# Attention and mixture-of-experts block on one core: value product in pieces of 256 queries, two query tiles less lag, last head's output kept in SBUF, more output projection inside the last head

## The chip, the cores and the metric

One NeuronCore of a Trainium2 chip runs the whole program. The metric is the device time of one execution in microseconds (us); the median of several executions counts. The engines run side by side and meet only at semaphores: TensorE (PE) multiplies matrices into PSUM, VectorE (DVE) and ScalarE (ACT) read PSUM and SBUF, GpSimd (POOL) reads and writes SBUF only, and SyncE (SP) issues DMAs. ACT and POOL issue DMAs too.

## The reference

2048 tokens of 256 features pass through an attention layer with 16 heads of 128 and through a layer of 8 experts with the best 2 chosen for each token. Cut to what matters:

```python
x = x + ln(attn(ln(x)))
x = x + ln(moe(ln(x)))

def attn(x):                       # codes * scales give the weights
    q, k, v = x @ Wq + bq, x @ Wk + bk, x @ Wv + bv       # 16 heads of 128
    p = softmax(q @ k.T / sqrt(128))                       # per head 2048 x 2048
    return concat_heads(p @ v) @ Wo + bo

def moe(x):                        # 8 experts, 176 hidden features each
    w = combine(top2(softmax(x @ Wr)))
    return sum_e w[:, e] * ((silu(x @ Wg[e]) * (x @ Wu[e])) @ Wd[e])
```

The result has to be accurate to float32, so each operand that is stored in 16 bits is stored twice, as a high part and as a low part (the rest), and a product is made of three: high by high, high by low, low by high.

## The kernel before

The order of the work on each engine is written out by hand: an instruction runs on its engine in the order in which the code emits it. SP's queue is such an order too, and a DMA that waits holds up those behind it.

**Start.** x is normalized, transposed and split; the first head's q, k and v projections begin. Projections write a PSUM bank of the tags "pj" or "pv" (`psA`, one bank each) or one of three "s" slots (`psS`). `proj_v(p, t0, n, tag, wide)` (L248 on) projects n tiles of V for head pair p. Without `wide` ACT copies the high part out of PSUM and DVE subtracts it from PSUM for the low part (L266, L267), so the bank stays taken until DVE is done. With `wide` ACT copies the bank to an SBUF tile `t32` (L274) and POOL makes both parts from that (L275, L276). `proj_qk` (L222 on; L237, L238, or L243 to L245) has the same two ways.

**Main loop.** A step g is one head h and one tile t of 128 queries: 16 x 16 = 256 steps and two more. In a step PE makes the scores of its tile in two halves (`scores_half`, L508 to L512, six matmuls of 512 columns each), DVE takes the maximum (L513, L517), ACT the exponentials p with their sums (L524). One step later DVE makes the reciprocal (L531, L534), ACT the scaled high part ph (L538), DVE the low part pl in two halves (L553). SP transposes ph and pl by DMA into `pth` and `ptl` (L541, L559), whose tiles hold four query tiles each, with two buffers of each.

**Value product.** For a head and a block b of 512 queries `pv_part` (L571 on) issues 48 matmuls of 512 columns into one PSUM bank, first the 32 that read `pth`, then the 16 that read `ptl`. They are cut into 8 units of 6, and each step runs two units (`pv_unit`). `PVLAG` (13) is the lag: unit u of the loop is unit u - PVLAG of the value product, so the first unit runs in step 6.5, and 9 units are left over when the loop ends. The finished bank goes through `t32` to POOL, which splits it into the tile `o` and writes it by DMA to `ot_d[b]` in DRAM (L594 to L599). Only the last head's last block is split by ACT and DVE.

**Fill.** At the end of a step `fill(h, t)` adds one projection for a coming head: q and k at even t, V at odd t. In the last head there is nothing left to project but three blocks of q.

**Output projection and the end.** `op_mm(b, half, js)` (L712 on) multiplies stored head outputs, read back with `load_oi` in groups of four heads (0.5 MB), by Wo: 16 matmuls of 256 columns for each group j. In the last head `early` and `late` place these loads on ACT's queue, the groups of block 0 between the steps, and the loads and splits of the gate weights. Block 0's layer norms (`ln_a`, `ln_b1`, `ln_b2`, `ln_c`, DVE and POOL) come after the loop, together with block 1's projection, block 0's router and the splits of the up and down weights. The slots for these loads, for V, K, ph, pl and the loaded weights all come from one pool of `NX` (21) slots with the tag "x".

**Feed-forward.** Four blocks of 512 tokens, each 11 chunks: gate and up products (`gate_up`, L987), then `down` (L1027). The layer norms and the router of a later block, and the projections of blocks 2 and 3, are placed between the chunks (`FIRST`, `PREP`, `PREP2`).

Of the kernel before, what the change touches and what calls it, by code (L numbers as in the profile page):

```python
# [32 lines left out]
PS = 16384.0  # L33
NX = 21


@with_exitstack
def sandwich(
# [26 lines left out]
    dram = ctx.enter_context(tc.tile_pool(name="dram", bufs=1, space=DRAM))  # L65
    ot_d = [dram.tile([128, 2, NH, 2, 256], HP, name=f"ot_d{b}") for b in range(4)]

# [427 lines left out]

    pt = pt_ctx.enter_context(tc.tile_pool(name="pt", bufs=2, reuse_waits="tile"))
    soft = soft_ctx.enter_context(tc.tile_pool(name="soft", bufs=2, reuse_waits="tile"))
# [38 lines left out]
    def high_part(h, t, m, p):  # L536
        ph = kqv.tile([128, S], HP, name="ph", tag="x", bufs=NX)
        nc.scalar.activation(ph, p, AF.Copy, scale=m[:, 6:7])  # L538
        if t % 4 == 0:
            PT[(h, t // 4)] = pt.tile([128, 4, 16, 128], HP, name="pth")  # L540
        nc.sync.dma_start_transpose(  # L541
            out=PT[(h, t // 4)][:, t % 4], in_=ph
        )
        return ph
# [3 lines left out]
    def low_half(half, h, t, m, p, ph):  # L548
        if half == 0:
            LOW[(h, t)] = kqv.tile([128, S], HP, name="pl", tag="x", bufs=NX)  # L550
        pl = LOW[(h, t)]
        cs = bass.ts(half, 1024)
        nc.vector.scalar_tensor_tensor(  # L553
            pl[:, cs], p[:, cs], m[:, 6:7], ph[:, cs], ALU.mult, ALU.subtract
        )
        if half == 1:
            if t % 4 == 0:
                PTL[(h, t // 4)] = pt.tile([128, 4, 16, 128], HP, name="ptl")
            nc.sync.dma_start_transpose(  # L559
                out=PTL[(h, t // 4)][:, t % 4], in_=LOW.pop((h, t))  # L560
            )
# [9 lines left out]
    def pv_part(h, b, e):  # L571
        if e == 0:
            pvps[(h, b)] = psA.tile([128, 512], F32, name="pv")
        ps = pvps[(h, b)]
        dc = bass.ts(h % 2, 128)
        for n in range(6 * e, 6 * e + 6):
            c, i = PV_ORDER[n]
            d = (PTL if i == 2 else PT)[(h, b)]
            nc.tensor.matmul(  # L579
                ps, V[(h // 2, c // 4)][:, i % 2, c % 4, dc], d[:, :, c, :],  # L580
                start=(n == 0), stop=(n == 47),
            )
        if e == 7:
            if (h, b) == (NH - 1, 3):
                o = kqv.tile([128, 2, 2, 256], HP, name="o_last", tag="x", bufs=NX)
                ps2 = halves(ps)
                nc.scalar.activation(o[:, :, 0, :], ps2, AF.Copy, scale=1.0 / PS)
                nc.vector.scalar_tensor_tensor(
                    o[:, :, 1, :], ps2, 1.0 / PS, o[:, :, 0, :], ALU.mult, ALU.subtract
                )  # L590
            else:
                o = soft.tile([128, 2, 2, 256], HP, name="o", bufs=1)
                t32 = soft.tile([128, 512], F32, name="t32")
                nc.scalar.activation(t32, ps, AF.Copy, scale=1.0 / PS)  # L594
                nc.gpsimd.tensor_copy(o[:, :, 0, :], halves(t32))
                nc.gpsimd.tensor_tensor(  # L596
                    o[:, :, 1, :], halves(t32), o[:, :, 0, :], ALU.subtract
                )
            nc.gpsimd.dma_start(  # L599
                out=ot_d[b][:, :, h].rearrange("p f l q -> p f (l q)"),  # L600
                in_=o.rearrange("p f l q -> p f (l q)"),
            )

    QK = {0: ("q", 0, 1), 2: ("k", 1, 0), 4: ("q", 0, 2), 6: ("k", 1, 1),
          8: ("q", 0, 3), 10: ("k", 1, 2), 12: ("q", 1, 0), 14: ("k", 1, 3)}

    LASTQ = {0: 1, 1: 2, 4: 3}

    def fill(h, t):
        p = h // 2  # L610
        if h == 0 and t < 6:
            proj_v(0, 4 + 2 * t, 2, "pv")
        if h == NH - 1:
# [72 lines left out]
    def load_oi(b, half, j, tag="x", eng=None):  # L686
        oi = kqv.tile(
            [128, 4, 2, 256], HP, name="oi", tag=tag, bufs=NX
        )
        (eng or nc.sync).dma_start(  # L690
            out=oi.rearrange("p h l q -> p (h l q)"),
            in_=ot_d[b][:, half, 4 * j : 4 * j + 4].rearrange("p h l q -> p (h l q)"),
        )
        OIN[(b, half, j)] = oi


    PVLAG = 13
    NS = NH * NT
# [13 lines left out]
    def op_mm(b, half, js, tag="pj", part=3):  # L712
# [9 lines left out]
        for j in js:  # L722
            oi = OIN.pop((b, half, j))
            for t in range(2):
                for hh in range(4):
                    for hl in range(2):
                        nc.tensor.matmul(  # L727
                            ps[:, t], oi[:, hh, hl, bass.ts(t, 128)],
                            wo[j // 2][:, 4 * (j % 2) + hh, :],
# [47 lines left out]
    def ln_c(b):  # L777
# [3 lines left out]
    XV = x.rearrange("b (c p t) d -> p (b c) t d", p=128, t=4)  # L781
    GW_LOAD = {2: 0, 4: 1, 6: 2, 8: 3}
    GW_SPLIT = {5: 0, 7: 1, 9: 2, 11: 3}
    OI_LOAD = {
        3: (0, 1, 0), 5: (0, 1, 1), 7: (0, 1, 2), 9: (1, 0, 0), 10: (1, 0, 1),
        12: (0, 0, 3), 13: (0, 1, 3), 14: (1, 0, 2),
    }
    OI_USE = {
        5: (0, (0,)), 6: (0, (1,)), 7: (0, (2,)), 8: (1, (0,)), 9: (1, (1,)), 10: (1, (2,)),
        14: (0, (3,)), 15: (1, (3,)),  # L790
    }

    def early(t):
# [9 lines left out]
        if t == 13:  # L803
            nc.gpsimd.tensor_tensor(crow, crow, brow, ALU.add)
        if t in (8, 10, 12):
            load_oi(0, 0, t // 2 - 4, eng=nc.scalar)

    def late(t):
# [5 lines left out]
        if t in OI_USE:  # L814
            op_mm(0, *OI_USE[t], "pj", 2)
        if t in GW_SPLIT:
# [4 lines left out]
        if t in OI_LOAD:  # L821
            load_oi(*OI_LOAD[t], eng=nc.scalar)
        if t == 11:
            X1[0] = kqv.tile([128, 4, D], F32, name="x1_0", tag="x", bufs=NX)
            nc.scalar.dma_start(out=X1[0], in_=XV[:, 0])


    defer = False
    prev2 = None
    for g in range(NS + 2):  # L830
        h, t = divmod(g, NT)
        live = g < NS
# [47 lines left out]
        if g == NS:  # L880
            ln_a(0)
        if g == NS + 1:
            load_oi(1, 0, 3)
            ust = [load_gu(wu, 0, kqv, "x", NX)]
            ust += [load_gu(wu, i, kqv, "x", NX) for i in range(1, 4)]
            ln_b1(0)
    UEND = 2 * (NS + 2)


    def tr(b, kc, tag="pj"):  # L890
        xn = AT[b]
        if kc == 0 and b == 0:
            XT[b] = [
                kqv.tile([128, 2, 512], F32R, name="xT0", tag="x", bufs=NX)
                for _ in range(2)
            ]
        elif kc == 0:
# [11 lines left out]
    def router_a(b, tag="pj"):  # L909
# [9 lines left out]
        if b == 0:  # L919
            LGT[b] = kqv.tile([8, 512], F32, name="lgT0", tag="x", bufs=NX)  # L920
        else:
# [24 lines left out]
    def router_c(b):  # L946
# [174 lines left out]
    op_mm(1, 0, (3,), "s")  # L1121
    for j in range(4):
        load_oi(1, 1, j)
    router_a(0, "s")
    for e in range(5, 7):
        pv_unit(UEND + e)
    split_gu(uw, 2, ust[2], True)
    router_b(0, "s")
    split_gu(uw, 3, ust[3], False)
    for e in range(7, 9):  # L1130
        pv_unit(UEND + e)
# [3 lines left out]
    router_c(0)  # L1135
# [101 lines left out]
```

## Time and profile before

| | |
|---|---|
| runs | 1825.22, 1827.94, 1835.36 us; median 1827.94 |
| profiled execution | 1829.47 us, its span 1827.6 us |
| mean granted PE clock | 0.994 |
| score matmuls (L508, L509, L512) | 3072 of 128x512, 379 ns each |
| value matmuls (L579) | 3072 of 128x512, 379 to 381 ns each |
| output projection matmuls (L727) | 512 of 128x256, 273 ns each |
| weight loads of the value product | 3072, 98 ns each |
| transposes on SP (L541, L559) | 256 and 256, 5.1 and 5.3 us from issue to landing (median) |
| reads of stored head outputs | 32 of 512 KB |

The profile of one execution gives for each engine its busy time, in groups of instructions by line, and in order of time. A matmul's duration there (379 ns) is longer than its share of the engine, since matmuls overlap; how fast PE works is read from the distance between starts. The page's second part cuts the span into 40 slices of some 46 us, one digit each for the busy share. A wait is told as the instruction that stood still, and the one that released it. The main loop runs from about 30 to 1560 us, the feed-forward from about 1590 to the end.

### The profile page before, as it was taken

The numbers are of one execution on the slowest core, as the hardware profiler recorded it, in microseconds if no ns is written. First come the engines' busy times: TensorE is split into PE (matmuls) and PEld (weight loads), VectorE is DVE, ScalarE is ACT, GpSimd is POOL, SyncE is SP. The second block draws the span as 40 slices with busy tenths as digits, with TensorE's granted clock in tenths as the row PEclk, the third lists the DMA queues.
The fourth block names the chain that finished last, engine by engine and source line by source line (L and its number), as shares of the span: only waits on it lengthen the run. The fifth ranks groups of instructions, "written<-read, shape, count | busy, mean of one in ns | idle before, by whom it ended". The sixth has DMA issues, their size and how long they took to land. (4 is left out here: it accounts for less than half of the span.)

```text
span 1827.6 us, 25508 instructions
## 1 busy us (share of the span) xinstructions
PE 1775.5 (97%) x8890; PEld 934.1 (51%) x8890; DVE 1631.0 (89%) x2269; ACT 1371.5 (75%) x1732; POOL 946.9 (52%) x915
## 2 busy tenths in 40 slices
PE   6899999999999999999999999999999998999997
PEld 4344444444444444444444444444444454688886
DVE  7999999999999999999999999999999987558666
ACT  5788888888888888888888888888888886322232
POOL 3396556555656565656565656566444332323232
PEclk9999999999999999999999999999999999999999
DMA  7999999999999999999999999999999999921000
GB/s 174 174 191 201 197 201 203 199 201 200 199 189 207 199 199 200 198 200 202 201 192 199 205 200 197 197 200 203 191 189 194 205 240 223 321 74 36 1 13 23
DMA packets 1092337, 330.70 MB, mean 181 GB/s; under 512 B 1069729, under 2 KB 1079281, under 8 KB 1092209
## 3 DMA queue, kind: packets, MB, share of 16 engines
q1 hardware_dynamic: 1077904, 293.29, 89.0%
q0 software_dynamic: 9920, 27.82, 5.5%
q10 hardware_dynamic: 4384, 7.96, 1.5%
q8 instruction: 70, 1.15, 0.2%
q14 instruction: 59, 0.48, 0.1%
HBM read 41.68 MB, written 18.87 MB: 33 GB/s over the span
## 5 line engine op out<-in xcount | busy, mean ns | idle before, releaser
L524 ACT ACTIVATE p<-s,m,ssc 128x1024 f32<-128x1024 f32 x512 | 612.2, 1200 | 190.5 <-DVE m L517 179.3
L553 DVE SCALAR_TENSOR_TENSOR pl<-p,m,ph 128x1024 f16<-128x1024 f32 x512 | 725.8, 1418 | 2.5 <-ACT ph L538 2.5
L513 DVE TENSOR_REDUCE m<-s 128x1 f32<-128x1024 f32 x512 | 622.3, 1216 | 39.8 <-PE s L512 38.2
L538 ACT ACTIVATE ph<-p,m 128x2048 f16<-128x2048 f32 x256 | 512.8, 2003 | 50.5 <-ACT t L243 15.3
L579 PE MATMUL pv<-pth,v 128*128 128x512 f16 x2048 | 507.7, 381 | 15.0 <-DMA pth<-ph 6.1
L579 PEld LDWEIGHTS <-v 128*128 128x128 f16 x3072 | 300.8, 98 | 383.5 <-issue 13.9
L508 PE MATMUL s<-kT,qT 128*128 128x512 f16 x1024 | 388.5, 379 | 2.7 <-ACT p L524 2.0
L509 PE MATMUL s<-kT,qT 128*128 128x512 f16 x1024 | 388.6, 379 | 0.7 <-POOL kT L245 0.7
L512 PE MATMUL s<-kT,qT 128*128 128x512 f16 x1024 | 304.6, 379 | 0.0
L579 PE MATMUL pv<-ptl,v 128*128 128x512 f16 x1024 | 251.9, 379 | 0.0
L244 POOL CAST qT<-t 128x512 f16<-128x512 f32 x63 | 78.5, 1245 | 236.4 <-ACT t L243 236.4
L275 POOL CAST v<-t 128x256 f16<-128x256 f32 (+1 forms) x105 | 47.1, 449 | 257.2 <-ACT t L274 257.2
L276 POOL TENSOR_TENSOR v<-t,v 128x256 f16<-128x256 f32 (+1 forms) x105 | 160.6, 1530 | 8.5
L512 PEld LDWEIGHTS <-qT 128*128 128x128 f16 x1024 | 100.3, 98 | 122.0 <-issue 1.5
L509 PEld LDWEIGHTS <-qT 128*128 128x128 f16 x1024 | 100.2, 98 | 113.7 <-issue 7.5
L508 PEld LDWEIGHTS <-qT 128*128 128x128 f16 x1024 | 100.3, 98 | 109.0 <-issue 1.0
L1002 POOL TENSOR_TENSOR hh<-sg,hh 128x512 fp32r<-128x512 f32 x42 | 55.1, 1311 | 143.5 <-ACT hh L1001 108.5
L1001 ACT CAST hh<-sg 128x512 fp32r<-128x512 f32 (+1 forms) x45 | 27.5, 612 | 107.0 <-DVE sg L1013 107.0
L524 ACT ACTIVATION_READ_ACCUMULATOR p<-s,m,ssc 128x1 f32 x512 | 99.0, 193 | 0.0
L596 POOL TENSOR_TENSOR o<-t,o 128x512 f16<-128x512 f32 x63 | 94.5, 1499 | 5.2
L244 POOL CAST kT<-t 128x512 f16<-128x512 f32 x60 | 64.5, 1075 | 58.5 <-ACT t L243 53.3
L245 POOL TENSOR_TENSOR kT<-t,kT 128x512 f16<-128x512 f32 x60 | 89.8, 1496 | 5.1
(189 smaller groups left out, 1833.4 us busy)
## 6 DMA issues: line engine op xcount, KB each, us to landing
ot_d<-o POOLq DMA_DIRECT2D x63, 256.0 KB, 4.2
oi<-ot_d SPq DMA_DIRECT2D x21, 512.0 KB, 8.8
oi<-ot_d ACTq DMA_DIRECT2D x11, 512.0 KB, 4.1
pth<-ph SPq DMA_TRANSPOSE x256, 5.1
ptl<-pl SPq DMA_TRANSPOSE x256, 5.3
xt<-in_L_attn_x SPq DMA_DIRECT2D x4, 512.0 KB, 4.7
woc<-in_L_attn_wo_codes SPq DMA_DIRECT2D x4, 512.0 KB, 9.6
wos<-in_L_attn_wo_scales SPq DMA_DIRECT2D x16, 128.0 KB, 8.4
```

The lines of the kernel that those rows point to most:

```text
L244: nc.gpsimd.tensor_copy(t[:, 0, :], t32)
L245: nc.gpsimd.tensor_tensor(t[:, 1, :], t32, t[:, 0, :], ALU.subtract)
L276: nc.gpsimd.tensor_tensor(v[:, 1, sl, :], t32, v[:, 0, sl, :], ALU.subtract)
L508: nc.tensor.matmul(s[:, j, :], q[:, 0, qc], k[:, 0, :], start=True, stop=False)
L509: nc.tensor.matmul(s[:, j, :], q[:, 0, qc], k[:, 1, :], start=False, stop=False)
L512: nc.tensor.matmul(s[:, j, :], q[:, 1, qc], k[:, 0, :], start=False, stop=True)
L513: nc.vector.tensor_reduce(m[:, half : half + 1], s, AX.XY, ALU.max)
L524: nc.scalar.activation(p[:, bass.ts(i, 1024)], s, AF.Exp, bias=m[:, 2:3], scale=ssc[:, 0:1], accum_out=m[:, 3 + i : 4 + i],)
L538: nc.scalar.activation(ph, p, AF.Copy, scale=m[:, 6:7])
L553: nc.vector.scalar_tensor_tensor(pl[:, cs], p[:, cs], m[:, 6:7], ph[:, cs], ALU.mult, ALU.subtract)
L579: nc.tensor.matmul(ps, V[(h // 2, c // 4)][:, i % 2, c % 4, dc], d[:, :, c, :], start=(n == 0), stop=(n == 47),)
L596: nc.gpsimd.tensor_tensor(o[:, :, 1, :], halves(t32), o[:, :, 0, :], ALU.subtract)
```

## The change

Six things are changed together.

- The value product works on 256 queries at a time: `pth` and `ptl` tiles hold two query tiles, with three buffers of each, and the 48 matmuls of a block become twice 48 of 256 columns, into the two halves of the same PSUM bank. A unit is 12 such matmuls. `PVLAG` goes from 13 to 9 units, two query tiles.
- The last head's output is not written to DRAM. It stays in four SBUF tiles (`O15`), and the fourth read-back group holds three heads instead of four.
- In the first head six of the eight V projections use `wide`. The V projections of later pairs are placed some steps earlier.
- In the last head the projection of block 0 is done by step 11, and half of block 1's follows in steps 12 to 15, with block 0's layer norms beside it in the same steps. Loads for them are placed earlier on ACT's queue.
- The other half of block 1 runs in the two steps after the scores have ended; block 2's projection moves from the feed-forward's first block to the stretch before it. The order of the stretch between loop and feed-forward is rewritten.
- The pool "x" has 22 slots. Block 0's router and its transposed input take three of them, cleared beforehand by POOL.

```diff
-NX = 21
+NX = 22
...
-    ot_d = [dram.tile([128, 2, NH, 2, 256], HP, name=f"ot_d{b}") for b in range(4)]
+    ot_d = [dram.tile([128, 2, NH - 1, 2, 256], HP, name=f"ot_d{b}") for b in range(4)]
...
-    pt = pt_ctx.enter_context(tc.tile_pool(name="pt", bufs=2, reuse_waits="tile"))
+    pt = pt_ctx.enter_context(tc.tile_pool(name="pt", bufs=3, reuse_waits="tile"))
...
-        if t % 4 == 0:
-            PT[(h, t // 4)] = pt.tile([128, 4, 16, 128], HP, name="pth")
+        if t % 2 == 0:
+            PT[(h, t // 2)] = pt.tile([128, 2, 16, 128], HP, name="pth")
...
-        for n in range(6 * e, 6 * e + 6):
+        f = e // 4
+        for n in range(12 * (e % 4), 12 * (e % 4) + 12):
             c, i = PV_ORDER[n]
-            d = (PTL if i == 2 else PT)[(h, b)]
+            d = (PTL if i == 2 else PT)[(h, 2 * b + f)]
             nc.tensor.matmul(
-                ps, V[(h // 2, c // 4)][:, i % 2, c % 4, dc], d[:, :, c, :],
-                start=(n == 0), stop=(n == 47),
+                ps[:, bass.ts(f, 256)], V[(h // 2, c // 4)][:, i % 2, c % 4, dc],
+                d[:, :, c, :], start=(n == 0), stop=(n == 47),
             )
         if e == 7:
+            if h == NH - 1:
+                o = kqv.tile([128, 2, 2, 256], HP, name="o_last", tag="x", bufs=NX)
+                O15[b] = o
+            else:
+                o = soft.tile([128, 2, 2, 256], HP, name="o", bufs=1)
...
-            nc.gpsimd.dma_start(
-                out=ot_d[b][:, :, h].rearrange("p f l q -> p f (l q)"),
-                in_=o.rearrange("p f l q -> p f (l q)"),
-            )
+            if h < NH - 1:
+                nc.gpsimd.dma_start(
+                    out=ot_d[b][:, :, h].rearrange("p f l q -> p f (l q)"),
+                    in_=o.rearrange("p f l q -> p f (l q)"),
+                )
...
+    V0 = (6, 8, 12, 14)
...
-        if h == 0 and t < 6:
-            proj_v(0, 4 + 2 * t, 2, "pv")
+        if h == 0 and t < 4:
+            proj_v(0, V0[t], 2, "pv", wide=soft)
+            if t == 1:
+                proj_v(0, 10, 2, wide=soft)
...
-            if t in (3, 5) and h > 0:
-                proj_v(p, 12 + (t - 3) // 2, 1, wide=soft)
-            elif t == 7 and h > 0:
-                proj_v(p, 14, 2, wide=soft)
-            elif t >= 9 and p + 1 < NH // 2:
-                proj_v(p + 1, (t - 9) // 2, 1, wide=soft)
+            if t == 1 and h > 0:
+                proj_v(p, 14, 1, wide=soft)
+            elif t == 3 and h > 0:
+                proj_v(p, 15, 1, wide=soft)
+            elif t >= 5 and p + 1 < NH // 2:
+                if h > 0 or t > 7:
+                    proj_v(p + 1, (t - 5) // 2, 1, wide=soft)
+                elif t == 7:
+                    proj_v(p + 1, 0, 2, wide=soft)
         elif p + 1 < NH // 2:
-            proj_v(p + 1, 4 + t // 2, 1, wide=soft)
+            proj_v(p + 1, 6 + t // 2, 1, wide=soft)
...
-    PVLAG = 13
+    PVLAG = 9
...
     OI_LOAD = {
-        3: (0, 1, 0), 5: (0, 1, 1), 7: (0, 1, 2), 9: (1, 0, 0), 10: (1, 0, 1),
-        12: (0, 0, 3), 13: (0, 1, 3), 14: (1, 0, 2),
+        3: (0, 0, 3), 4: (0, 1, 3), 9: (1, 0, 0), 10: (1, 0, 1), 11: (1, 0, 2), 12: (1, 0, 3),
+        13: (1, 1, 0), 14: (1, 1, 1), 15: (1, 1, 2),
     }
     OI_USE = {
-        5: (0, (0,)), 6: (0, (1,)), 7: (0, (2,)), 8: (1, (0,)), 9: (1, (1,)), 10: (1, (2,)),
-        14: (0, (3,)), 15: (1, (3,)),
+        5: (0, 0, (0,)), 6: (0, 0, (1,)), 7: (0, 0, (2,)), 8: (0, 1, (0,)), 9: (0, 1, (1,)),
+        10: (0, 1, (2,)), 11: (0, 0, (3,)),
+        12: (1, 0, (0,)), 13: (1, 0, (1,)), 14: (1, 0, (2,)), 15: (1, 0, (3,)),
     }
...
+            if t == 11:
+                op_mm(0, 1, (3,), "pj", 2)
...
+        LN0 = {12: ln_a, 13: ln_b1, 14: ln_b2, 15: ln_c}
+        if t in LN0:
+            LN0[t](0)
...
                 proj_v(0, 2, 2, "pv")
+                proj_v(0, 4, 2, "s", wide=soft)
...
+        if g >= NS:
+            op_mm(1, 1, ((0, 1), (2, 3))[g - NS], "s")
...
         if g == NS:
-            ln_a(0)
+            for j in range(4):
+                load_oi(2, 0, j)
...
-    op_mm(1, 0, (0, 1, 2), "s")
-    ln_b2(0)
-    split_gu(uw, 0, ust[0], True)
-    ln_c(0)
-    for e in range(1, 5):
-        pv_unit(UEND + e)
     tr(0, 0, "s")
     tr(0, 1, "s")
+    pv_unit(UEND + 1)
+    router_a(0, "s")
+    pv_unit(UEND + 2)
+    router_b(0, "s")
+    split_gu(uw, 0, ust[0], True)
+    op_mm(2, 0, (0, 1, 2, 3), "s")
...
-    op_mm(1, 1, (0, 1), "s")
     router_d(0, "s")
     split_d(*d1)
-    op_mm(1, 1, (2, 3), "s")
+    op_mm(2, 1, (0, 1, 2, 3), "s")
...
-        3: [lambda: op_pass(2, 0, "pv")],
-        5: [lambda: tr(1, 0), lambda: op_pass(2, 1, "pv"), lambda: loads(3, 7)],
+        5: [lambda: tr(1, 0), lambda: loads(3, 7)],
```

More of the change, by code (lines that the diff above doesn't have):

```diff
@@ L538, in high_part @@
         nc.scalar.activation(ph, p, AF.Copy, scale=m[:, 6:7])
-        if t % 4 == 0:
-            PT[(h, t // 4)] = pt.tile([128, 4, 16, 128], HP, name="pth")
+        if t % 2 == 0:
+            PT[(h, t // 2)] = pt.tile([128, 2, 16, 128], HP, name="pth")
         nc.sync.dma_start_transpose(
-            out=PT[(h, t // 4)][:, t % 4], in_=ph
+            out=PT[(h, t // 2)][:, t % 2], in_=ph
         )
@@ L556, in low_half @@
         if half == 1:
-            if t % 4 == 0:
-                PTL[(h, t // 4)] = pt.tile([128, 4, 16, 128], HP, name="ptl")
+            if t % 2 == 0:
+                PTL[(h, t // 2)] = pt.tile([128, 2, 16, 128], HP, name="ptl")
             nc.sync.dma_start_transpose(
-                out=PTL[(h, t // 4)][:, t % 4], in_=LOW.pop((h, t))
+                out=PTL[(h, t // 2)][:, t % 2], in_=LOW.pop((h, t))
             )
     pvps = {}
+    O15 = {}
     def halves(t):
@@ L575, in pv_part @@
         dc = bass.ts(h % 2, 128)
-        for n in range(6 * e, 6 * e + 6):
+        f = e // 4
+        for n in range(12 * (e % 4), 12 * (e % 4) + 12):
             c, i = PV_ORDER[n]
-            d = (PTL if i == 2 else PT)[(h, b)]
+            d = (PTL if i == 2 else PT)[(h, 2 * b + f)]
             nc.tensor.matmul(
-                ps, V[(h // 2, c // 4)][:, i % 2, c % 4, dc], d[:, :, c, :],
-                start=(n == 0), stop=(n == 47),
+                ps[:, bass.ts(f, 256)], V[(h // 2, c // 4)][:, i % 2, c % 4, dc],
+                d[:, :, c, :], start=(n == 0), stop=(n == 47),
             )
         if e == 7:
+            if h == NH - 1:
[3 more added lines that the diff above has]
+                o = soft.tile([128, 2, 2, 256], HP, name="o", bufs=1)
             if (h, b) == (NH - 1, 3):
-                o = kqv.tile([128, 2, 2, 256], HP, name="o_last", tag="x", bufs=NX)
                 ps2 = halves(ps)
@@ L591, in pv_part @@
             else:
-                o = soft.tile([128, 2, 2, 256], HP, name="o", bufs=1)
                 t32 = soft.tile([128, 512], F32, name="t32")
@@ L686, in load_oi @@
     def load_oi(b, half, j, tag="x", eng=None):
-        oi = kqv.tile(
-            [128, 4, 2, 256], HP, name="oi", tag=tag, bufs=NX
-        )
+        n = 4 if j < 3 else 3
+        oi = kqv.tile([128, n, 2, 256], HP, name="oi", tag=tag, bufs=NX)
         (eng or nc.sync).dma_start(
             out=oi.rearrange("p h l q -> p (h l q)"),
-            in_=ot_d[b][:, half, 4 * j : 4 * j + 4].rearrange("p h l q -> p (h l q)"),
+            in_=ot_d[b][:, half, 4 * j : 4 * j + n].rearrange("p h l q -> p (h l q)"),
         )
-        OIN[(b, half, j)] = oi
-    PVLAG = 13
+        OIN[(b, half, j)] = [oi[:, hh] for hh in range(n)]
+    PVLAG = 9
     NS = NH * NT
@@ L723, in op_mm @@
             oi = OIN.pop((b, half, j))
+            if j == 3:
+                oi.append(O15[b][:, half])
             for t in range(2):
@@ L727, in op_mm @@
                         nc.tensor.matmul(
-                            ps[:, t], oi[:, hh, hl, bass.ts(t, 128)],
+                            ps[:, t], oi[hh][:, hl, bass.ts(t, 128)],
                             wo[j // 2][:, 4 * (j % 2) + hh, :],
@@ L781, in sandwich @@
     XV = x.rearrange("b (c p t) d -> p (b c) t d", p=128, t=4)
-    GW_LOAD = {2: 0, 4: 1, 6: 2, 8: 3}
+    EARLY = {
+        4: (0, 0, 0), 6: (0, 0, 1), 8: (0, 0, 2), 10: (0, 1, 0), 12: (0, 1, 1), 14: (0, 1, 2),
+    }
+    GW_LOAD = {0: 0, 2: 1, 6: 2, 8: 3}
     GW_SPLIT = {5: 0, 7: 1, 9: 2, 11: 3}
     OI_LOAD = {
-        3: (0, 1, 0), 5: (0, 1, 1), 7: (0, 1, 2), 9: (1, 0, 0), 10: (1, 0, 1),
-        12: (0, 0, 3), 13: (0, 1, 3), 14: (1, 0, 2),
+        3: (0, 0, 3), 4: (0, 1, 3), 9: (1, 0, 0), 10: (1, 0, 1), 11: (1, 0, 2), 12: (1, 0, 3),
+        13: (1, 1, 0), 14: (1, 1, 1), 15: (1, 1, 2),
     }
     OI_USE = {
-        5: (0, (0,)), 6: (0, (1,)), 7: (0, (2,)), 8: (1, (0,)), 9: (1, (1,)), 10: (1, (2,)),
-        14: (0, (3,)), 15: (1, (3,)),
[3 rows of a table added]
     }
@@ L804, in early @@
             nc.gpsimd.tensor_tensor(crow, crow, brow, ALU.add)
-        if t in (8, 10, 12):
-            load_oi(0, 0, t // 2 - 4, eng=nc.scalar)
+        if t in EARLY:
+            load_oi(*EARLY[t], eng=nc.scalar)
     def late(t):
@@ L814, in late @@
         if t in OI_USE:
-            op_mm(0, *OI_USE[t], "pj", 2)
+            b = OI_USE[t][0]
+            op_mm(*OI_USE[t], "pj", 2 if b == 0 else 3)
+            if t == 11:
+                op_mm(0, 1, (3,), "pj", 2)
         if t in GW_SPLIT:
@@ L822, in late @@
             load_oi(*OI_LOAD[t], eng=nc.scalar)
-        if t == 11:
+        if t == 15:
+            load_oi(1, 1, 3, eng=nc.scalar)
+        if t == 7:
             X1[0] = kqv.tile([128, 4, D], F32, name="x1_0", tag="x", bufs=NX)
             nc.scalar.dma_start(out=X1[0], in_=XV[:, 0])
+        LN0 = {12: ln_a, 13: ln_b1, 14: ln_b2, 15: ln_c}
+        if t in LN0:
+            LN0[t](0)
     defer = False
@@ L880, in sandwich @@
         if g == NS:
-            ln_a(0)
+            for j in range(4):
+                load_oi(2, 0, j)
+        if g == NS - 1:
+            rt0 = kqv.tile([128, 1024], F32, name="rt0", tag="x", bufs=NX)
+            xt0 = [
+                kqv.tile([128, 2, 512], F32R, name="xT0", tag="x", bufs=NX)
+                for _ in range(2)
+            ]
+            for z in (rt0, *xt0):
+                nc.gpsimd.memset(z.bitcast(F32), 0.0)
         if g == NS + 1:
[L883 to L886, printed above, removed]
+            ust = [load_gu(wu, i, kqv, "x", NX) for i in range(4)]
     UEND = 2 * (NS + 2)
@@ L892, in tr @@
         if kc == 0 and b == 0:
[L893 to L896, printed above, removed]
+            XT[b] = xt0
         elif kc == 0:
@@ L919, in router_a @@
         if b == 0:
-            LGT[b] = kqv.tile([8, 512], F32, name="lgT0", tag="x", bufs=NX)
+            LGT[b] = rt0[:8, :512]
         else:
@@ L957, in router_c @@
         )
-        cx = tl.tile([128, 4, 8, 16], F32, name="cx", tag="sg", bufs=3)
+        if b == 0:
+            cx = rt0[:, 512:].rearrange("p (t e r) -> p t e r", t=4, e=8)
+        else:
+            cx = tl.tile([128, 4, 8, 16], F32, name="cx", tag="sg", bufs=3)
         sx = [128, 4, 8, 16]
@@ L1111, in sandwich @@
     d1 = load_d(4)
-    op_mm(1, 0, (0, 1, 2), "s")
-    ln_b2(0)
-    split_gu(uw, 0, ust[0], True)
-    ln_c(0)
-    for e in range(1, 5):
-        pv_unit(UEND + e)
     tr(0, 0, "s")
     tr(0, 1, "s")
+    pv_unit(UEND + 1)
[4 more added lines that the diff above has]
+    op_mm(2, 0, (0, 1, 2, 3), "s")
     split_gu(uw, 1, ust[1], False)
-    op_mm(1, 0, (3,), "s")
+    split_gu(uw, 2, ust[2], True)
+    split_gu(uw, 3, ust[3], False)
     for j in range(4):
[L1123 to L1131, printed above, removed]
+        load_oi(2, 1, j)
+    pv_unit(UEND + 3)
+    router_c(0)
+    pv_unit(UEND + 4)
     pt_ctx.close()
@@ L1134, in sandwich @@
     dw = tl.tile([128, 2, NCH, D], F32R)
-    router_c(0)
     split_d(*d0)
     load_x1(1)
-    op_mm(1, 1, (0, 1), "s")
     router_d(0, "s")
     split_d(*d1)
-    op_mm(1, 1, (2, 3), "s")
+    op_mm(2, 1, (0, 1, 2, 3), "s")
     ln_a(1)
@@ L1173, in sandwich @@
     FIN = {2: fin1, 3: fin2}
-    loads(2)
     for q in range(4 * NCH + 2):
```

## The prediction

> **What bounds the kernel now.** I read busy shares first, then slices, the PE timeline at both ends, the waits, and last SP's timeline.
>
> ```profile
> PE 1775.5 (97%) x8890; PEld 934.1 (51%) x8890; DVE 1631.0 (89%) x2269; ACT 1371.5 (75%) x1732; POOL 946.9 (52%) x915
> ...
> PE   6899999999999999999999999999999998999997
> ...
> DVE  7999999999999999999999999999999987558666
> ```
>
> A busy PE need not be a full PE, so I look at spacing. In the windows view PE is busy 99.4 to 99.7 of every 100 us from 400 to 1400, and in the timeline six score and six value matmuls that start at 1520.42 give way to the next scores at 1523.01: 2.59 us for 12, so 215.8 ns each, with nothing between. In the middle every PE instruction added lengthens the kernel. DVE at 95% (190.4 of 200 us) is next. Time can be won only where PE stands still, and that is at the two ends and in one small recurring wait.
>
> At the start the PE timeline shows (start, duration, [idle before <- releaser]):
>
> ```profile
> 46.48 1.05 PE L255 MATMUL pj<-wv,xnT 128*128 128x256 bf16 x8 [1.97 <-DVE v L267]
> ...
> 53.11 1.83 PE L255 MATMUL pj<-wv,xnT 128*128 128x256 bf16 x8 [2.13 <-DVE v L267]
> ...
> 60.55 1.05 PE L255 MATMUL pj<-wv,xnT 128*128 128x256 bf16 x8 [2.13 <-DVE v L267]
> ...
> 73.42 1.47 PE L579 MATMUL pv<-pth,v 128*128 128x512 f16 x6 [1.10 <-DVE v L267]
> ```
>
> The V projection of each early tile waits until DVE has subtracted the one before out of the same PSUM bank, and no value product exists before 73.42. The eight idle stretches from 40.24 to 73.42 sum to 11.35 us. After the one at 53.11 PE runs slow for ten rows of matmuls: 1.62 us for 8 where 0.88 is usual, then 2.23 us for 6 scores where 1.29 is usual, another 1.7. Lost: **13.0 us**.
>
> At the other end:
>
> ```profile
> 1538.86 0.59 PE L512 MATMUL s<-kT,qT 128*128 128x512 f16 x2
> 1545.06 4.31 PE L579 MATMUL pv<-pth,v 128*128 128x512 f16 x12 [5.60 <-DMA pth<-ph]
> ...
> 1560.01 5.40 PE L727 MATMUL op_s<-wo,oi 128*128 128x256 bf16 x48
> 1567.83 7.03 PE L579 MATMUL pv<-pth,v 128*128 128x512 f16 x24 [2.41 <-issue]
> ```
>
> 5.60, 2.41 and three small ones (0.31, 0.85, 0.59) are 9.8 us; the 12 and the 24 matmuls behind the long gaps take 4.14 and 6.86 us to the next start where 2.59 and 5.18 are usual, 3.2 more. Lost: **13.0 us**. Why so late? SP's timeline:
>
> ```profile
> 1529.23 6.72 SPq L541 DMA_TRANSPOSE pth<-ph  x1
> 1536.05 2.72 SPq L559 DMA_TRANSPOSE ptl<-pl  x1
> 1538.87 3.30 SPq L541 DMA_TRANSPOSE pth<-ph  x1
> ```
>
> Counting back from the last one (1561.76, tile 15), the transpose at 1538.87 is tile 11's. ACT had written that ph by 1527.01, so SP is 12 us behind. From 1490 to 1538.87 SP is never free and takes 6.1 us a tile, while PE takes only 5.2 us for tiles without projection. So the transposes, beside one 0.5 MB load per tile, are what the last head runs into. "issue" at 1567.83 is, I think, the same: tile 15's transpose went out at 1561.76 and needs the usual 5 to 6 us.
>
> The recurring wait, from the waits of PE:
>
> ```profile
> PE pv L579 <- POOL v L276: 5.0, 7, 0.8
> ...
> PE pv L579 <- POOL v L275: 0.4, 1, 0.4
> ```
>
> The last V tiles of each head pair come 0.7 us too late: **5.4 us**.
>
> **The change part by part.**
>
> 1. Value product by 256. 3072 matmuls of 512 columns become 6144 of 256, each with its own weight load. Nearest row: the output projection (L727), 128x256 with a load for every matmul; 64 of them take 7.00 us in the chain of waits, 16 take 1.74 to 1.75 us in the last head. That is 109.1 ns, so a pair costs 218.2 against 215.8: 2.4 ns x 3072 = **+7.4 us**, all on PE's path. The Trainium skill speaks against this ("TensorE: Matmul & The Clock Gate", Back-to-back issue gap): in a stream of load and matmul pairs it counts about 81 ns at 128 columns where a lone matmul needs 56, because the load wants its share. That 25 ns on 256 columns would make 134 ns and +161 us (estimate from that page). The row has the same pairs at 109.1, with the load (98 ns each) hidden, and the page's 131 ns for 512 columns is not this trace's 215.8 either. I take the row. Ends: +5 (108.7 ns) to +43 us (115 ns).
>
> 2. Start. Six of the eight V projections go through ACT and POOL, so the bank is free after ACT's copy (0.58) and DVE loses 0.68 us a tile. Then the loop of exponentials 2.4, m and reciprocal 0.5, pl 1.2, reduce 1.2, maximum 0.3 gives 5.5 us a tile instead of 6.2 to 7.4 (ACT's exponentials now start at 41.71, 47.96, 54.59, 62.03). One more projection ahead of the first scores delays them 0.9. POOL gets 6 x (1.05 + 1.65) = 16.1 us, beside q and k splits of 2.6 each and weight loads; from 34 to 62 I count some 27 us, so it just keeps up. The last V tile is needed at about 66. The first value unit moves from step 6.5 to 4.5 (a step is one query tile), to about 57.5. From there PE is full: 0.86 + 5.18 + 0.86 + 4 units of 1.30 reach the old 73.42 at 69.6, so 3.8 earlier, with 4 units (5.2 us) already done. **-9.0 us**; ends -4 (POOL holds up the shared t32) and -12.
>
> 3. V of later pairs is projected so that its last tile has 1.6 steps (9 us) to its use instead of 1.0 (5.8, and 0.7 short). **-5.4 us**; ends 0 and -6. Transposes keep two steps to their first use, and those of the low part get 2.8 steps instead of 4. A third buffer frees each pair's space one step ahead. No new PE wait in the middle.
>
> 4. Last head. The projection in it grows from 8 to 12 groups of 16 matmuls (1.75 us each): PE work moved, zero by itself. But tiles 5 to 15 then last at least 6.95 us on PE, more than SP's 6.1 us, so the backlog drains rather than grows; the load at each tile from 9 on is what SP had beside it before. Head 15's write and read-back fall away; they were off the path except through DMA traffic. Two groups of 32 (3.5 us each) now stand between the last scores and tile 15's values, which PE reaches 17.6 us after the last scores (six units of 1.3, a group of 1.75, 1.1 of transposes for the router, and twice 3.5). Maximum 1.5, exponentials 2.4, reciprocal 0.4, ph 2.0 and a transpose of 5 to 9 give 11 to 15. Against it, block 0's normalization moves onto DVE: at, stats, ln_b1 3.6, ln_b2 2.2, ln_c 2.4, together 13.5 us over five tiles of 5.4 (DVE from 1518.15 to 1523.80, less 0.29 idle). DVE then needs 40.5 us where PE needs 36.5: 4 us late, and ln_c and the last statistics stand directly before tile 15's reciprocal (up to 4). On ACT's queue the last loads may also wait for a slot that a transpose must free, and ph waits behind them; four loads stand before tile 15's low transpose on SP, covered by 7 us of projection. I let 5 of the 13.0 remain: **-8.0 us**; ends -13 and +3.
>
> 5. Feed-forward. Its first block loses op_pass(2), 14 us of cover; DVE there has 2.1 us per chunk plus normalizations of 3.6, 2.2 and 2.4 in three chunks, 14.5 against PE's 12.5. **+1 us**; ends 0 and 3.
>
> Sum: 7.4 - 9.0 - 5.4 - 8.0 + 1.0 = **-14.0 us**. The profiled execution took 1829.5 (span 1827.6 and 1.9 around it), which gives 1815.5; the median of the runs is 1.5 lower, so for a median I say **1814**.
>
> **Rivals.**
> - The end does not pay: DVE or a slot takes the place of the late transpose. For it: 40.5 against 36.5 us, and the loads on ACT. Against it: the two projection groups before tile 15's values. 1814 + 8 = **1822**. Chance 0.2.
> - Start and V pay half, because ACT and DVE's loop of 5.5 us is so near PE's 5.8: 1814 + 7 = **1821**, with half of the end gone too 1825. Chance 0.09.
> - Slower: the 256-column matmuls in the main loop space wider than in L727, where the load has only 11 ns to hide in. The price is 6.1 us per ns. The other parts bring 21.4 us, so it decides from 111.4 ns; at 115 ns +43.6 - 21.4 gives **1850**. Against it: spacing in every L727 row but one. Chance 0.16, with 1835 to 1860 as its span.
>
> **How the numbers follow.** The forecast has 0.55 (1806 to 1820); less than 0.5%, 9 us, can't be told from no change. Below 1819: nearly all of the forecast and a little of the rivals, 0.56. Up to 1837: the first two rivals, 0.27. The rest, 0.17, is the slow one with an end that fails as well. Leaving out most of that rival: 1804 to 1834.
>
> **What would show it.** PE's value rows x6144 with 218 ns a pair; no "DVE v" wait of PE after 40 us and a first value matmul near 58; "POOL v" gone from PE's waits; no 5 us gap before pv near the end and SP less than 6 us behind ACT; PE idle from the last scores to the first gup below 5 us. A pair above 223 ns, or a gap over 9 us around the last scores, makes the forecast wrong.

## The result, and the profile after

The changed kernel takes **1833.93 us** in the median of 22 runs (1827.89 to 1841.51), the kernel before 1828.18 (22 runs on the same chip). The ratio is 1.0030, with a 95% interval from 1.0016 to 1.0043: 5.5 us slower, where 14 us faster was forecast. The time lies just inside the stated 1804 to 1834, at its far end, and on the wrong side of the kernel before. The profiled execution has a span of 1832.3 us, 4.7 more than that of before.

Busy time and the PE and DVE slices of the changed kernel's page:

```profile
PE 1783.5 (97%) x11962; PEld 1237.5 (68%) x11962; DVE 1631.3 (89%) x2263; ACT 1372.8 (75%) x1738; POOL 964.0 (53%) x938
...
PE   7999999999999999999999999999999999899997
...
DVE  7999999999999999999999999999999888568666
```

3072 more matmuls are there, and PE is busy 8.0 us longer. The weak slice near the end is still there, only one slice later.

**The start** is as the prediction described it. PE's timeline of the changed kernel (start, duration, [idle before <- releaser]):

```profile
51.15 0.38 PE L508 MATMUL s<-kT,qT 128*128 128x512 f16 x1 [2.64 <-ACT p L524]
...
58.96 1.47 PE L581 MATMUL pv<-pth,v 128*128 128x256 f16 x12
61.56 1.47 PE L581 MATMUL pv<-pth,v 128*128 128x256 f16 x12
```

The first value matmul stands at 58.96 instead of 73.42, and no projection waits for DVE. What PE waits for now is the exponentials.

**The middle and the end** in one view, the waits of PE:

```profile
PE pv L581 <- DMA pth<-ph: 11.5, 12, 2.0
...
PE pct_s L1006 <- DVE rt L994: 5.9, 1, 5.9
PE s L508 <- ACT p L524: 4.6, 6, 2.6
PE op_s L740 <- DMA oi<-ot_d: 2.8, 1, 2.8
```

(Total, times, longest.) The waits for `POOL v` are gone. In their place stands one that the loop of before hardly had, value matmuls that wait for a transposed tile: 12 times here, once between 90 and 1500 us before:

```profile
PE pv L579 <- DMA pth<-ph: 0.5, 1, 0.5
```

All 12 are in the loop, and each stands at the first unit of a block's second half.

One of them, in PE's timeline:

```profile
138.25 1.47 PE L581 MATMUL pv<-ptl,v 128*128 128x256 f16 x12
...
142.65 1.47 PE L581 MATMUL pv<-pth,v 128*128 128x256 f16 x12 [1.64 <-DMA pth<-ph]
```

SP's timeline of the same stretch, in which a row is one DMA's issue,

```profile
128.71 3.93 SPq L541 DMA_TRANSPOSE pth<-ph  x1
132.74 3.15 SPq L559 DMA_TRANSPOSE ptl<-pl  x1
135.99 3.78 SPq L541 DMA_TRANSPOSE pth<-ph  x1
139.86 3.19 SPq L559 DMA_TRANSPOSE ptl<-pl  x1
```

and the row of ACT's timeline that wrote the tile which PE is waiting for:

```profile
128.94 2.00 ACT L538 ACTIVATE ph<-p,m 128x2048 f16<-128x2048 f32 x1
```

The tile that PE needs at 141.01 was finished by ACT at 130.94. SP had only just begun the tile before it (128.71), then had that tile's low part to issue, and came to this one at 135.99. Issuing took 3.78 us and the landing 2.9 more. PE's unit was due 10.1 us after `ph`; the data needed 11.7.

**The end** in PE's timeline:

```profile
1574.68 1.46 PE L740 MATMUL op_s<-wo,oi 128*128 128x256 bf16 x6 [2.82 <-DMA oi<-ot_d]
...
1593.71 1.91 PE L581 MATMUL pv<-ptl,v 128*128 128x256 f16 x16
1601.52 1.11 PE L1006 MATMUL pct_s<-ident,rt 128*128 128x128 f32 x4 [5.90 <-DVE rt L994]
```

At 1593.71 PE runs the last value unit that is left; behind it stands the router's transpose, which needs `rt` from DVE. DVE's timeline of the same stretch:

```profile
1593.04 0.75 DVE L751 SCALAR_TENSOR_TENSOR at<-op_s,sig,crow 128x512 f32<-128x512 f32 x1 [5.73 <-PE op_s L740]
...
1595.09 3.16 DVE L675 TENSOR_TENSOR uw<-gu_raw,uw 128x704 fp32r<-128x704 f32 x2 [0.29 <-ACT uw L673]
1598.16 2.32 DVE L982 TENSOR_TENSOR cw<-iota,ixf 128x64 f32<-128x64 f32 x1
...
1600.77 0.69 DVE L994 TENSOR_TENSOR rt<-cw 128x512 f32<-128x512 f32 x1
```

and SP's:

```profile
1579.04 5.72 SPq L559 DMA_TRANSPOSE ptl<-pl  x1
1584.87 3.35 SPq L682 DMA_DIRECT2D gu_raw<-in_L_ffn_Wu  x4
```

Read backwards: `rt` waits on DVE behind the split of the up weights (`uw`), which waits for ACT's copy, which waits for a load that SP could issue only at 1584.87, behind tile 15's low transpose. The indices that `router_c` reads were complete on DVE at 1587.30.

### The profile page after: what moved, and what is told of

It is laid out like the page before. It is cut to its first block, busy times and chain, and to the rows that moved or that the text cites. A ratio compares the mean times of both kernels' runs of the same rounds, so it can differ in the third digit from the quotient of the medians.

```text
span 1832.3 us, 31565 instructions
## 1 busy us (share of the span) xinstructions
PE 1783.5 (97%) x11962; PEld 1237.5 (68%) x11962; DVE 1631.3 (89%) x2263; ACT 1372.8 (75%) x1738; POOL 964.0 (53%) x938
## 5 line engine op out<-in xcount | busy, mean ns | idle before, releaser
L581 PEld LDWEIGHTS <-v 128*128 128x128 f16 x6144 | 601.3, 98 | 191.3 <-issue 10.8
L581 PE MATMUL pv<-pth,v 128*128 128x256 f16 x4096 | 510.3, 273 | 11.6 <-DMA pth<-ph 11.5
L581 PE MATMUL pv<-ptl,v 128*128 128x256 f16 x2048 | 265.1, 273 | 0.0
L244 POOL CAST kT<-t 128x512 f16<-128x512 f32 x60 | 79.2, 1319 | 236.2 <-ACT t L243 236.2
L275 POOL CAST v<-t 128x256 f16<-128x256 f32 (+1 forms) x117 | 57.6, 492 | 276.2 <-ACT t L274 276.2
L276 POOL TENSOR_TENSOR v<-t,v 128x256 f16<-128x256 f32 (+1 forms) x117 | 170.6, 1458 | 9.5
L245 POOL TENSOR_TENSOR qT<-t,qT 128x512 f16<-128x512 f32 x63 | 90.6, 1438 | 5.3
L243 ACT ACTIVATE t<-pj,bqs 128x512 f32<-128x512 f32 x123 | 83.8, 682 | 1.3 <-PE pj L230 1.3
```

The source lines that it names most:

```text
L245: nc.gpsimd.tensor_tensor(t[:, 1, :], t32, t[:, 0, :], ALU.subtract)
L276: nc.gpsimd.tensor_tensor(v[:, 1, sl, :], t32, v[:, 0, sl, :], ALU.subtract)
L581: nc.tensor.matmul(ps[:, bass.ts(f, 256)], V[(h // 2, c // 4)][:, i % 2, c % 4, dc], d[:, :, c, :], start=(n == 0), stop=(n == 47),)
```

## The experiments

The medians below are of 6 to 22 runs, each beside runs of the kernel before on the same chip. The ratio is always to the kernel before; the changed kernel's is 1.0030.

**e1, the split alone.** The kernel before with nothing changed but the 256 columns, half after half; tiles of four and the lag stay. The second half's units come when all of V is long there, the first half's need the last V tiles earlier, so those are projected two steps earlier.

```diff
-        for n in range(6 * e, 6 * e + 6):
+        f = e // 4
+        for n in range(12 * (e % 4), 12 * (e % 4) + 12):
...
-                ps, V[(h // 2, c // 4)][:, i % 2, c % 4, dc], d[:, :, c, :],
+                ps[:, bass.ts(f, 256)], V[(h // 2, c // 4)][:, i % 2, c % 4, dc],
+                d[:, 2 * f : 2 * f + 2, c, :],
...
-            if t in (3, 5) and h > 0:
-                proj_v(p, 12 + (t - 3) // 2, 1, wide=soft)
-            elif t == 7 and h > 0:
+            if t in (1, 3) and h > 0:
+                proj_v(p, 12 + (t - 1) // 2, 1, wide=soft)
+            elif t == 5 and h > 0:
```

> The kernel before, with its lag of 13 units and its four-tile transposed buffers, but each value product issued as 256-column matmuls for one half of the block after the other, and the last four V tiles of a pair projected two steps earlier because the third unit now reads them. Theory (the split costs its 2.5 ns a pair and nothing else): PE +7.7 us, and the 5.4 us that PE waited for V are gone, so +2 us, and PE waits for pth under 2 us in the middle. Rival (closely packed loads and matmuls cost more in the long run than their spacing shows): +10 us or more, with PE idle on 'issue'.

Measured: 1826.84 us, ratio 0.9994 (0.9985 to 1.0004), span 1825.4. From 90 to 1500 us PE waits for one thing, once:

```profile
PE s L509 <- POOL kT L245: 0.7, 1, 0.7
```

That is 1.1 us faster by the ratio, where 2 us slower was expected. So twice as many weight loads cost no more than their 2.5 ns a pair here, and V two steps earlier suffices to take the `POOL v` waits away.

**e2, the rest without split, lag and later pairs' V.** The changed kernel with 512 columns, tiles of four in two buffers, a lag of 13 units, 21 slots, and V of later pairs as before. Nine units are left over at the end, the last five behind `router_c`.

```diff
-        if t % 2 == 0:
-            PT[(h, t // 2)] = pt.tile([128, 2, 16, 128], HP, name="pth")
+        if t % 4 == 0:
+            PT[(h, t // 4)] = pt.tile([128, 4, 16, 128], HP, name="pth")
...
-    PVLAG = 9
+    PVLAG = 13
...
     router_c(0)
-    pv_unit(UEND + 4)
+    for e in range(4, 9):
+        pv_unit(UEND + e)
```

> The changed kernel with 512-column matmuls, four-tile buffers and lag 13 put back (and the V placement of later pairs and the slot count of before); start, last head and end stay as changed. Theory (the middle's new waits for pth belong to the smaller pieces; start is worth 7 us, the end nothing): against the kernel before the start keeps about 4 us (the 5.2 us of lag are given back but the early V waits stay away), V waits stay, so -2 to -6 us. Rival (the transposes themselves limit the loop and start gains are given back there): 0 +- 2 us.

Measured: 1822.94 us, ratio 0.9977 (0.9968 to 0.9986). That is 4.2 us faster by the ratio, as expected: the start and the last head together do pay when the lag stays. PE's waits from 1500 us to the first gate product fall from 9.2 us in the kernel before to 1.7. From 90 to 1500 us `POOL v` is back (4.3 and 0.4), `pth` costs 2.1, and the largest wait is a new one, for the exponentials:

```profile
PE s L508 <- ACT p L524: 7.4, 6, 1.9
```

Four of the six, 6.5 us, stand between 1435 and 1500 us, in the last two heads, where the kernel before has none. e5, e7, e8 and e9 have 3.5 to 5.3 us of it between 1420 and 1510 us too. What delays the exponentials there was not tried.

**e3, the unit behind the projection.** In my own reading of the trace (blocks 4 to 55, each block's or half's first unit) the time from the end of `ph` to its transpose's landing, and to the unit that reads it, is on average:

| kernel, unit | `ph` to landing | `ph` to use | left over | kept PE waiting |
|---|---|---|---|---|
| before | 8.10 us | 10.79 us | 2.70 us | 1 of 52 |
| after, first half | 8.47 | 11.13 | 2.65 | 0 |
| after, second half | 8.78 | 10.22 | 1.44 | 7, 5.1 us |

The loop of before puts a block's first unit behind the step's projection; the changed one does so for the first half only. e3 does it for the second half too.

```diff
-        first = live and (2 * g + 1 - PVLAG) % 8 == 0
+        first = live and (2 * g + 1 - PVLAG) % 4 == 0
```

> The changed kernel with one edit: the fifth unit of a block, which is the first to read the second pair of tiles, is placed behind the step's projection, as the first unit already is. Theory (that unit came 0.86 us too early for its transpose): PE's waits for pth in the middle fall from 11.5 us to under 4, and the time falls by 6 to 8 us against the changed kernel, to about -1 us against the kernel before. Rival (SP's transposes, 5.4 to 5.7 us of issue in a step of 5.9, are the bound): the waits come back at other units and the time stays within 2 us of the changed kernel, +5 against before.

Measured: 1836.95 us (7 runs), ratio 1.0047 (1.0030 to 1.0064): not faster, and whether it is slower than the changed kernel the two intervals leave open. The theory fell. The use moved from 10.22 to 11.06 us as meant, but the landing moved as well, from 8.78 to 9.58, and 1.48 us were left over. Waits of PE:

```profile
PE pv L581 <- DMA pth<-ph: 8.7, 10, 2.7
...
PE pct_s L1006 <- DVE rt L994: 7.2, 1, 7.2
```

One candidate for the reason stands in SP's own waits between 90 and 1500 us. There low transposes wait for value matmuls, it seems for a buffer that these still read: in e3 seven times, in the changed kernel twice.

```profile
SPq L559 <- PE pv L581: 21.6, 7, 5.0
```

```profile
SPq L559 <- PE pv L581: 4.7, 2, 2.9
```

That this moved the landings is not shown. The end lost 1.3 us more than in the changed kernel, at the same place.

**e4, the router's last part earlier.** `router_c` runs straight behind `router_b`, ahead of the up weights' split.

```diff
     router_b(0, "s")
+    router_c(0)
     split_gu(uw, 0, ust[0], True)
...
     pv_unit(UEND + 3)
-    router_c(0)
     pv_unit(UEND + 4)
```

> The changed kernel with one edit: block 0's combine weights (router_c) are emitted right behind router_b, ahead of the up-weight splits and the statistics of block 2 on DVE. Theory: the 5.9 us in which PE waited for them, and the slow clock behind it (1.2 us), go; next late are the loads for block 2's second half, issued at 1593 to 1597 and used at 1602, so -3 to -6 us against the changed kernel. Rival (those loads are just as late): 0 to -1 us, with PE idle at the same place on a DMA.

Measured: 1829.13 us, ratio 1.0007 (0.9999 to 1.0015), 4.2 us of span less than the changed kernel, as expected. The wait for `rt` (5.9 us) is gone. Another wait of PE, for a load, is 2.3 us longer than in the changed kernel; it stands ahead of the place of the edit:

```profile
1577.12 1.46 PE L740 MATMUL op_s<-wo,oi 128*128 128x256 bf16 x6 [5.09 <-DMA oi<-ot_d]
```

**e5, one tile of lag given back.** The changed kernel with `PVLAG` 11; seven units are left over.

```diff
-    PVLAG = 9
+    PVLAG = 11
...
-    pv_unit(UEND + 4)
+    for e in range(4, 7):
+        pv_unit(UEND + e)
```

> The changed kernel with a lag of 11 units instead of 9 (one query tile more), the two further units left over placed behind the others. Theory (at lag 9 the second pair of a block is read 10.2 us after its ph, and its transpose lands 8.8 us after it on average, so any late one stops PE; and the end lost the units that covered its chains): one step more, 5.9 us, takes the pth waits in the middle from 11.5 us to under 1; 2.6 us more of idle at the start; two more units cover the end. In sum -8 to -11 us against the changed kernel, so -2 to -5 against the kernel before. Rival (transposes are the loop's bound): PE's waits move to scores or stay, within 2 us of the changed kernel, +5 against before.

Measured: 1825.47 us, ratio 0.9985 (0.9973 to 0.9996): 8.5 us less than the changed kernel by the medians, 8.2 by the ratios. The theory held in the main, though 4.2 us of `pth` are left where under 1 was expected. No first unit of blocks 4 to 55 waits any more; `ph` to use is 16.8 and 16.3 us, 4.7 and 4.4 are left over. The two `pth` waits that remain from 90 to 1500 us stand at 1416 and 1465 us, in the last two heads:

```profile
PE pv L581 <- DMA pth<-ph: 4.2, 2, 2.1
PE s L508 <- ACT p L524: 3.6, 3, 2.4
```

The first value matmul comes at 63.56 us, and `pct_s` still waits 4.59 us for DVE.

**e6, the start alone.** The kernel before with `wide` in the first head.

```diff
-        if h == 0 and t < 6:
-            proj_v(0, 4 + 2 * t, 2, "pv")
+        if h == 0 and t < 4:
+            proj_v(0, (6, 8, 12, 14)[t], 2, "pv", wide=soft)
+            if t == 1:
+                proj_v(0, 10, 2, wide=soft)
...
                 proj_v(0, 2, 2, "pv")
+                proj_v(0, 4, 2, "s", wide=soft)
```

> The kernel before with one part of the change: six of the first head's eight V projections through ACT and POOL, one of them ahead of the first scores. No lag, split or end is changed. Theory: DVE's hold on the bank (9.3 us of PE's waits) goes, but the loop of exponentials, reciprocal, pl and maximum stays at 5.5 us a tile and the first value product stays at step 6.5, so PE waits for exponentials instead: first value matmul at 69 to 71 instead of 73.4, time -2 to -4 us. Rival (the start's idle is hidden by later waits on transposes): 0 us.

Measured: 1824.24 us, ratio 0.9985 (0.9978 to 0.9993), some 2.7 us faster. The first value matmul came at 71.88 us, a little later than the 69 to 71 expected. PE's timeline:

```profile
68.22 0.58 PE L508 MATMUL s<-kT,qT 128*128 128x512 f16 x1 [3.60 <-ACT p L524]
...
71.88 1.46 PE L579 MATMUL pv<-pth,v 128*128 128x512 f16 x6
```

Faster V alone brings PE to the next wait, the exponentials; value work moved forward by the lag is what fills it.

**e7, e2 with V two steps earlier.** No split, the old lag, all else; against e2:

```diff
-            if t in (3, 5) and h > 0:
-                proj_v(p, 12 + (t - 3) // 2, 1, wide=soft)
-            elif t == 7 and h > 0:
+            if t in (1, 3) and h > 0:
+                proj_v(p, 12 + (t - 1) // 2, 1, wide=soft)
+            elif t == 5 and h > 0:
```

> The changed kernel with 512 columns and lag 13 put back, as in the run before of that kind, and V of each pair's last four tiles projected two steps earlier. Theory (each part of the change but split and lag is worth its time): PE's waits for V (4.7 us) go and nothing takes their place, since transposes there have the margin of the kernel before: -8 to -10 us against the kernel before (ratio 0.995). Rival: the waits turn into waits for pth or for exponentials, -4 us as without that edit (0.998).

Measured: **1818.24 us, ratio 0.9958 (0.9943 to 0.9973)**, the best of all and faster than both kernels. From 90 to 1500 us no value matmul waits for V, and the three kinds of wait that there are sum to 6.1 us:

```profile
PE s L508 <- ACT p L524: 4.4, 5, 2.8
PE pv L580 <- ACT ph L538: 1.0, 1, 1.0
PE s L509 <- POOL kT L245: 0.7, 1, 0.7
```

The one of a value matmul (at 1428.73 us) is put down to `ph`, the last event before it. But the transposed tile that this matmul reads, issued at 1423.61, landed 4.9 us later, only 0.25 us before the matmul began, so most of the 1.0 us may belong to `pth`.

**e8, e5 and e4 together.** Lag 11 and the early `router_c`; against the changed kernel:

```diff
-    PVLAG = 9
+    PVLAG = 11
...
     router_b(0, "s")
+    router_c(0)
```

> The changed kernel with lag 11 and router_c emitted right behind router_b. Theory: beside what lag 11 brings, DVE's late combine weights no longer stop PE; with two more units as cover for block 2's loads the end loses less than 4 us: -10 to -14 us against the changed kernel, -4 to -8 against before. Rival (loads of block 1 and 2 are as late as the weights): within 2 us of lag 11 alone.

Measured: 1819.62 us, ratio 0.9960 (0.9946 to 0.9975). The whole split version, with one tile of lag and one placement changed, is 7.4 us faster than the kernel before. PE's longest gap at the end:

```profile
1567.10 0.83 PE L740 MATMUL op_s<-wo,oi 128*128 128x256 bf16 x6 [2.90 <-DMA oi<-ot_d]
```

**e9, e7 with the split put back,** half after half as in e1, lag 13; against e7:

```diff
-        for n in range(6 * e, 6 * e + 6):
+        f = e // 4
+        for n in range(12 * (e % 4), 12 * (e % 4) + 12):
...
-                ps, V[(h // 2, c // 4)][:, i % 2, c % 4, dc], d[:, :, c, :],
+                ps[:, bass.ts(f, 256)], V[(h // 2, c // 4)][:, i % 2, c % 4, dc],
+                d[:, 2 * f : 2 * f + 2, c, :],
```

> The version of e7 (tiles of four queries, lag of 13 units, nine units left over) with one thing put back: the value product by 256 queries, half after half. Theory (the split costs only its 2.5 ns per pair of matmuls, and what went wrong in the changed kernel is the shorter lag): 7.7 us slower than e7, so 1.5 us faster than before to 1 us slower, around 1826; PE's waits between 90 and 1500 us show no pth; no gap over 3 us from 1555 us to the first gate product. Rival (the split itself unsettles the loop or the end, whatever the lag): 12 us or more slower than e7, so at or above the changed kernel's 1834, with pth waits or a gap before pct_s of 4 us or more.

Measured: 1826.09 us, ratio 0.9989 (0.9976 to 1.0002). That is 7.9 us above e7 by the medians (5.7 by the two ratios) and 7.8 below the changed kernel (7.5 by the ratios). From 90 to 1500 us there is no `pth`, and `pct_s` does not wait; from 1555 us to the first gate product the longest gap is 0.49 us:

```profile
1576.45 0.41 PE L943 MATMUL rp_s<-xT,rw 128*8 128x512 f32 x1 [0.49 <-ACT xT L932]
...
1602.35 1.64 PE L1018 MATMUL gup<-xT,gw 128*128 128x512 f32 x6
```

The first gate product of the changed kernel starts at 1610.59. So from the best version to the changed one there are two steps of about equal size: the split, 6 to 8 us, and the shorter lag with its tiles of two, third buffer, slot and V's places to match, 8.

## Why the prediction was wrong

**What bounds the kernel: right.** PE does in the middle, and only PE's idle time could be won.

**Step 1, the split: right.** Twelve matmuls that start at 58.96 give way at 60.27, so a pair takes 218.3 ns, which is also the median of 466 such groups in the loop; 2.5 ns x 3072 = 7.7 us where +7.4 was said. The doubled loads stay hidden, as the row said and against the rule it was weighed with. e1, and e9 against e7, show about that or less by themselves, so the slower rival, wider spacing, did not happen.

**Step 2, the start: right mechanism, too large.** Six waits of PE from 38 to 70 us sum to 4.4 us and slow matmuls (granted clock 0.50 from 51.9 to 55.3 us) to about 1.4, 5.8 against 13.0 before: -7.2 where -9.0 was said. The mis-sized term is "5.5 us a tile": ACT's exponentials start at 42.31, 49.81, 55.46, 61.11 and 67.46, so 7.50, 5.65, 5.65 and 6.35. The 7.50 is where PE's wait of 2.64 comes from. The rival in which start and V pay half has its reason in the same loop; of the start it took a fifth.

**Step 3, V of later pairs: the step that failed.** V came in time, worth its 5.4 us. But "No new PE wait in the middle" was wrong: `pth` costs 11.5 us from one end of the loop to the other, where the loop of before lost 7.3 in all small waits: +4.8 instead of -5.4. Behind the longest of these waits PE was slow as well:

```profile
1444.52 2.73 PE L581 MATMUL pv<-pth,v 128*128 128x256 f16 x12 [2.03 <-DMA pth<-ph]
1447.05 1.49 PE L230 MATMUL pj<-xnT,wk 128*128 128x512 f16 x4
```

The granted clock was 0.50 from 1444.6 to 1448.0 us; the twelve took 2.53 us to the next start instead of 1.31, the four 1.33 instead of 0.87. That is another 1.7, so this part came to +6.5.

The working counted steps: two from a tile to its first use, before and after. It did not count microseconds. From the end of `ph` to the use two steps are 10 to 11 us, and the trace of before already had a tile on its way for 8.1 of them, with SP issuing for 5.5 of every 5.9 us. 2.7 us were to spare on average. The first use of a second half was new, came 0.6 us earlier and had 1.4 to spare, and there all the waits stand. e5, with tiles of two and three buffers kept, shows that the lag decides: with one step more these waits are gone from the loop up to 1416 us, and two are left in the last two heads. In the changed kernel 4.7 of the 11.5 us stand in these heads too; e2 has 2.1 us there with the old lag, so not all of that part need be the lag's. The low part, which lost more steps in the prediction's own count, never became the wait.

**Step 4, the last head: the other one.** Nothing instead of -8.0. Gaps of 0.91, 2.82 and 5.90 us and slow matmuls of about 3 (granted clock 0.50 from 1574.3 to 1577.7 and from 1598.2 to 1605.0 us) make 12.7. The 13.0 of before took in a wait of 0.59 us at 1602.32 that stands behind the first gate product; by the same count it is 12.4. The transpose that had been late is no longer the cause (tile 15's goes out at 1574.46, 4.4 us behind ACT's `ph`); the first rival's picture, DVE and a load in its place, is what came. Two things were missing in the sum. One is that the chain from tile 15's low transpose through SP, a load, ACT and DVE to `rt` has work on PE in front of it only as long as value units are left: nine before, five after. That is the lag's second price. e5, with seven units, still shows this gap, at 4.6 us; e9, with nine, shows neither this gap nor the one before `op_s`; e4, which takes `rt` out of the chain, wins 4.2 us of span. The other is a load for block 1 on ACT's queue: issued at 1562.8 and landed 11.8 us later, beside the transposes, where the median of these loads is 5.1.

**Step 5, the feed-forward: nothing instead of +1.** 14.0 us of projection moved ahead of it; the first gate product is 18.7 us later than before, and the span 4.7 longer, so the feed-forward gave back what was moved, to within 0.1.

All together: with each distance between matmul starts held against the median of its kind, there are 7.6 us more of work. What is lost beyond that changes by -1.2 ahead of the first scores, -7.5 from there to 90 us, +6.3 to 1500 us, -0.3 to the first gate product and +0.1 behind it. That is +4.9, against 4.7 between the spans. The -1.2 is not the change's doing: 1.1 of it is a wait at L428, 3.3 us in the profiled execution of the kernel before and 2.2 in all the others, e1 with the same start among them.

The forecast's time was 20 us too low although part of its gains is real. e6 shows that the start pays 2.7 us, e7 against e2 that the earlier V pays 4.7 by the medians (3.5 by the ratios). For the last head with its output in SBUF and the projection in it, e2 against e6 leaves 1.3 us, which the intervals do not separate from nothing: the waits that went from the end are met by new ones in the last two heads, in e2 6.5 us for exponentials and 2.1 for `pth`. The lag of two tiles less was taken as free, and it is the part that runs against the others. Whether one tile of it is worth having is not settled: e8 lies 6.5 us below e9 by the medians, but with `router_c` moved as well, and e5, without that move, is level with e9.

## What to carry to other kernels

A lag is a margin in microseconds, not in steps: before shortening it, measure in the trace how long the slowest producer takes from its input's end to its landing, and how far that spreads. Here the queue in between issued for nine tenths of a step, and how far it stood behind differed by some 3 us between two executions of the same loop. And the work that a lag leaves over at a loop's end is cover for the next stage's chains; when it is consumed earlier, ask what had stood behind it.

## What was not expected of the hardware

**A small VectorE instruction held up by GpSimd.** The first `cw` of `router_c` takes 0.22 us in the kernel before, 0.21 in e9 and 2.32 in the changed kernel. Before:

```profile
1586.68 0.22 DVE L951 TENSOR_TENSOR cw<-iota,ixf 128x64 f32<-128x64 f32 x1
```

In the changed kernel POOL is at work on a split when `cw` begins:

```profile
1597.26 3.13 POOL L675 TENSOR_TENSOR dw<-draw,dw 128x1024 fp32r<-128x1024 f32 x1 [1.51 <-ACT dw L673]
```

It ends at 1600.39, and `cw`, from 1598.16, ends at 1600.48. In e3 POOL's split ends at 1599.06 and `cw` (2.31 us) at 1599.14. In the other nine runs `cw` takes 0.20 to 0.22 us, and no such split of POOL's is running when it begins. The Trainium skill (SBUF — State Buffer, SBUF: two separate sides) says that VectorE with two inputs in SBUF and a GpSimd instruction that reads SBUF exclude each other for a whole instruction; `cw` has two such inputs, and these numbers agree. It is 2.1 of the 5.90 us of that wait.

**The same loop with two backlogs.** e5 and e8 run the same main loop, yet the transposes had 4.7 and 4.4 us left over in the one and 7.6 and 7.9 in the other; from `ph` to the end of SP's issue it was 9.3 and 8.8 us against 6.2 and 5.4. Each is one profiled execution. e4 and the changed kernel share a loop as well, and there 2.55 and 1.42 us were left over against 2.65 and 1.44. So at a lag of 9, where PE waits for late tiles, two executions agree; at 11 they do not, and a margin read from one trace there is less certain than its digits look.
